# Half of the last block of an expert's second weights, loaded one step early and copied in place, in the expert loop of a GNN and mixture-of-experts kernel

## The chip, the cores and the metric

The kernel runs on one core of a Trainium2 chip. The metric is the device time of one execution in microseconds (us); lower is better. The work is in float32.

## The reference, cut to what matters

A two-layer graph attention network is added to 625 rows of 768 features. Then come causal attention and a mixture of eight experts, of which each row uses one (K = 1, so its gate weight is 1). Only the last part is touched by the change:

```python
h2 = _ln(x, ln2_g, ln2_b).reshape(-1, d)
gate_logits = h2 @ Wg
w, sel = jax.lax.top_k(gate_logits, K)              # K = 1
...
hid = jax.nn.relu(jnp.einsum('nd,edf->enf', h2, W1) + b1[:, None, :])   # 768 -> 3072
y = jnp.einsum('enf,efd->end', hid, W2) + b2[:, None, :]                # 3072 -> 768
moe = jnp.einsum('ne,end->nd', combine, y)
return x + moe.reshape(b, t, d)
```

## The kernel before, in words

**Rows by expert.** After attention, each of five tiles of 125 rows is normalised, its expert chosen, and its rows are scattered by expert into two DRAM buffers: `xg` (the normalised rows) and `xr` (the sum so far, and the row's number). The expert that most rows of the first tile chose is the first expert; its weights are loaded and its first 128 rows are worked on in a step written out ahead of the loop (step A), between whose products the last routing work runs.

**The table.** About forty small VectorE operations on one partition then make a table of 21 columns with four rows: expert, whether it is new, kind of step, first row in `xg` and `xr`. A step has kind 0, 1 or 2 for M = 128, 64 or 32 rows. An expert's rows are cut into at most one step of 32, at most one of 64 and then some of 128, in that order. The engines read the words they need from the table at the start of a loop step (`values_load`), and branch on the kind with `tc.If`, so the code of a step is there three times.

**One step** (`step`, L1075). P = 128 / M groups of hidden columns are worked on side by side. `into(c)` (L1091) multiplies the turned rows `xbT` with a chunk of W1 into PSUM `ph`, and VectorE copies it to `hb` (L1095). `turn(c)` (L1102) transposes it on TensorE, and ScalarE adds the bias and applies ReLU into `hbT` (L1107). `out_of(c)` (L1114) multiplies `hbT` with a chunk of W2 and accumulates in PSUM `py`, for two halves i of 384 output columns. TensorE's order is written out by hand (`manual_schedule`). For M = 64 and M = 32 there are n = 3 chunks, and it is: into 0, into 1, turn 0, into 2, turn 1, out 0, turn 2, (transposes `tpx` of the next step's rows, L891) out 1, (more `tpx`) out 2. In a step of 32, `out_of(c)` has K = 2 slices of 128 hidden rows for each of 4 groups; group g reads slices 2g and 2g + 1 of block c. So its first two products read the first half of `w2[c]`, and the third and the fourth the second half. After the last product VectorE adds `py` to `yo` (which holds `xr`'s rows plus the bias b2, L1156 to L1158) at L1166, and GpSimd scatters `yo` to the output (L1168).

**The weights.** W1 and W2 of an expert lie in SBUF once, each as three blocks, `w1[0..2]` and `w2[0..2]`, of 3 MB; there is no second buffer. `load_expert(e, new)` (L1066) is called at the end of a step for the next step's expert: twelve transfers of 1.5 MB, two for each block (L1037 for W1, L1031 for W2), with the bias b2 (L1043) in the middle, all on SyncE's queue in the order w1[0], w1[1], w1[2], b2b, w2[0], w2[1], w2[2]. Where the next step has the same expert, the condition `new` is 0: SyncE still goes through the instructions and their waits, and no bytes move. Each transfer waits until TensorE has read the old contents, and for the eighth transfer before it on the same queue (eight completion semaphores are used in turn). SyncE's order is written out by hand as well.

**Per step on the other queues.** GpSimd loads the next step's rows (`xb`, L1340, always 128 rows) and this step's sums (`rb`, L1058, always 128 rows), and VectorE copies the step's first-layer bias (L1064).

The lines that matter most, of `out_of` and of the adds at the end:

```python
for k in range(K):
    for i in range(2):
        for g in range(P):
            mm = nc.tensor.matmul(py[g * M:(g + 1) * M, i, :384], hbT[c][:, k, g * M:(g + 1) * M],
                                  w[:, o + g * K + k, i * 384:(i + 1) * 384], ...)
...
for g in range(P):
    for cc in range(4 // P):
        nc.vector.tensor_add(yv[:, :, cs], yv[:, :, cs], py[g * M:(g + 1) * M, :, cs])
```

Of the kernel before, what the change touches and what calls it, by code (L numbers as in the profile page):

```python
# [9 lines left out]
F32 = mybir.dt.float32  # L10
F16 = mybir.dt.float16
BF16 = mybir.dt.bfloat16
I32 = mybir.dt.int32
# [11 lines left out]
D = 768  # L25
# [37 lines left out]
def gnn_moe_kernel(ctx: ExitStack, tc: tile.TileContext, p, out):  # L63
# [83 lines left out]
    with tc.tile_pool(name="gnn", bufs=1) as gp:  # L147
# [322 lines left out]
        sx = ctx.enter_context(tc.tile_pool(name="sx", bufs=1, side="right", reuse_waits="tile"))  # L470
# [214 lines left out]
    table = keep.tile([1, 4, NS + 1], I32, name="table")  # L685
    first = keep.tile([1, 1], I32, name="first")
    sxt = ctx.enter_context(tc.tile_pool(name="sxt", bufs=1, side="right", reuse_waits="tile"))
# [339 lines left out]

    def load_piece(e, l, c, **cond):
        if l:
            for k in range(0, FC // 128, 4):  # L1030
                nc.sync.dma_start(  # L1031
                    w2[c][:, k:k + 4, :],
                    W2[ds(e, 1), c * FC + k * 128:c * FC + (k + 4) * 128, :]
                    .rearrange("o (k p) d -> p (o k) d", p=128), **cond)
        else:
            for k in range(0, KD, 3):
                nc.sync.dma_start(  # L1037
                    w1[c][:, k:k + 3, :],
                    W1[ds(e, 1), k * 128:(k + 3) * 128, c * FC:(c + 1) * FC]
                    .rearrange("o (k p) f -> p (o k) f", p=128), **cond)  # L1040

    def load_bias(e, **cond):
        nc.sync.dma_start(b2b, b2[ds(e, 1), :].to_broadcast([B, D]), **cond)  # L1043
# [12 lines left out]
    def sums_so_far(row):  # L1056
        rb = mw.tile([B, D + 1], F32, name="rb", bufs=1)
        nc.gpsimd.dma_start(rb, xr[ds(row, B), :])  # L1058
        return rb

    def biases(e):
        bT = mw.tile([128, NK], F32, name="bT")
        of_e = bT_all.rearrange("p (e k) -> p e k", k=NK)[:, ds(e, 1), :]
        return bT, nc.vector.tensor_copy(bT, of_e.rearrange("p o k -> p (o k)"))  # L1064

    def load_expert(e, new):  # L1066

        with tc.manual_schedule(engines={SP}):
            for l in range(2):
                for c in range(NFC):  # L1070
                    load_piece(e, l, c, cond=new)
                if not l:
                    load_bias(e, cond=new)

    def step(M, xT, bT, rb, after=None):  # L1075
# [33 lines left out]
        def out_of(c):  # L1109
            w, o = (w2[c // 2], (c % 2) * K) if P == 1 else (w2[c], 0)  # L1110
            for k in range(K):
                for i in range(2):
                    for g in range(P):
                        mm = nc.tensor.matmul(  # L1114
                            py[g * M:(g + 1) * M, i, :384], hbT[c][:, k, g * M:(g + 1) * M],
                            w[:, o + g * K + k, i * 384:(i + 1) * 384],
                            start=(c == 0 and k == 0), stop=(c == n - 1 and k == K - 1))
            return mm
# [43 lines left out]
        for g in range(P):  # L1162
            for cc in range(4 // P):
                w = 384 * P // 4
                cs = slice(cc * w, (cc + 1) * w)
                nc.vector.tensor_add(yv[:, :, cs], yv[:, :, cs], py[g * M:(g + 1) * M, :, cs])  # L1166
# [138 lines left out]
    v.tensor_copy(tabf[:, 0, :NS], its_number)  # L1305
    v.tensor_copy(table, tabf)
# [8 lines left out]
    row_0 = nc.values_load(table[0:1, 3, 0:1], engines=[pool], min_val=0, max_val=NR - B)  # L1315
    first_rows = nc.gpsimd.dma_start(xb, xg[ds(row_0, B), :])
    first_turned, = step_a

    def next_expert(i):
        return (nc.values_load(table[0:1, 0, ds(i, 1)], engines=[SP], min_val=0, max_val=E - 1),  # L1320
                nc.values_load(table[0:1, 1, ds(i, 1)], engines=[SP], min_val=0, max_val=1))

    load_expert(*next_expert(0))

    def all_of(step, e, new):
        with tc.manual_schedule(engines={PE}):
            for _ in step:
                pass
        load_expert(e, new)
# [3 lines left out]
    with tc.For_i(0, n_blk, 1, iteration_sync="reg_based") as i:  # L1333
        e = nc.values_load(table[0:1, 0, ds(i, 1)], engines=[mybir.EngineType.DVE], min_val=0,
                           max_val=E - 1)
        kind = nc.values_load(table[0:1, 2, ds(i, 1)], min_val=0, max_val=2)
        row, row_next = (nc.values_load(table[0:1, 3, ds(k, 1)], engines=[pool], min_val=0,
                                        max_val=NR - B) for k in (i, i + 1))

        nc.gpsimd.dma_start(xb, xg[ds(row_next, B), :])  # L1340
        rb = sums_so_far(row)
        bT, s = biases(e)
        tc.add_manual_dep(s.ins, first_rows.ins.name, ORDER)

        then = next_expert(i + 1)
        with tc.If(kind == 0) as cmp:
            all_of(step(B, xbT, bT, rb, first_turned), *then)
        with cmp.Else():
            with tc.If(kind == 1) as cmp2:
                all_of(step(64, xbT, bT, rb, first_turned), *then)  # L1350
            with cmp2.Else():
                all_of(step(32, xbT, bT, rb, first_turned), *then)
# [31 lines left out]
```

## Time and profile before

| what | value |
|---|---|
| time, three runs | 1070.33, 1070.99 (median), 1072.49 us |
| the profiled execution's own time | 1070.6 us |
| its span in the profile | 1067.9 us |
| TensorE busy | 1006.7 us (94% of the span) |
| VectorE, ScalarE, GpSimd busy | 451.7, 319.0, 57.1 us |
| step A | from 627.9 us |
| the expert loop | 700.1 to 1060 us |
| bytes moved by DMA | 194.48 MB, mean 182 GB/s |

The steps of the loop, from TensorE's timeline (start of the first `into` product) and from the times at which transfers of weights run. "New" means that the step's expert was not the expert of the step before, so that its weights were loaded during the step before:

| step | rows M | starts (us) | weights |
|---|---|---|---|
| 1 | 64 | 700.13 | as in step A |
| 2 | 128 | 736.35 | the same |
| 3 | 64 | 801.68 | new, loaded in step 2 |
| 4 | 32 | 840.54 | new, loaded in step 3 |
| 5 | 128 | 866.12 | the same |
| 6 | 64 | 931.47 | new, loaded in step 5 |
| 7 | 32 | 965.72 | new, loaded in step 6 |
| 8 | 64 | 993.27 | the same |
| 9 | 32 | 1027.52 | new, loaded in step 8 |

How to read it: the page's slices show how busy each engine was over the span, and the granted TensorE clock. A group row gives busy time and mean duration, then the idle time ahead of it on its engine and what ended that. A timeline row gives start, duration, engine, line, operation, tiles, shapes, count, and in brackets the idle time before it with its releaser. The engine named SPq is SyncE's sequencer, which issues the transfers of weights.

### The profile page before, as it was taken

How to read it: one execution, taken by the hardware profiler on the slowest of the kernel's cores; microseconds unless marked ns; L12 is line 12 of the kernel's file. 1: busy time of each engine (PE TensorE's matmuls, PEld its weight loads, DVE VectorE, ACT ScalarE, POOL GpSimd, SP SyncE). 2: the span in 40 equal slices, each digit the busy share in tenths (PEclk: the TensorE clock that was granted, in tenths of full speed). 3: DMA queues.
4: the chain of work that ended last, by engine and by line, in shares of the span. 5: the costliest groups of instructions: out<-in, count | busy, mean ns of one | idle time of the engine just before them, and what ended most of it. 6: DMA issues, size and time to landing. Idle time of an engine off the chain costs nothing. (4 is left out here: it accounts for less than half of the span.)

```text
span 1067.9 us, 14435 instructions
## 1 busy us (share of the span) xinstructions
PE 1006.7 (94%) x4763; PEld 574.8 (54%) x4764; DVE 451.7 (42%) x1264; ACT 319.0 (30%) x817; POOL 57.1 (5%) x97
## 2 busy tenths in 40 slices
PE   6889999999999999999999999999999889998993
PEld 4455465677656556666665654544453435533341
DVE  6886786484284910665438544011101121011211
ACT  6677553452231111444435211110202112021120
POOL 1200100000000100000001101000000000000000
PEclk9999999999999999999999999999999899998997
DMA  9300500301300347998002679012799948899693
GB/s 286 129 1 1 181 9 0 133 1 43 93 14 0 103 120 220 398 389 293 1 2 63 237 251 351 12 46 58 304 321 387 408 177 322 294 413 409 248 412 153
DMA packets 85669, 194.48 MB, mean 182 GB/s; under 512 B 32397, under 2 KB 34068, under 8 KB 85609
## 3 DMA queue, kind: packets, MB, share of 16 engines
q1 hardware_dynamic: 79817, 174.00, 44.3%
q0 software_dynamic: 5712, 19.54, 5.3%
q8 instruction: 36, 0.59, 0.2%
q10 hardware_dynamic: 80, 0.16, 0.1%
q14 instruction: 24, 0.20, 0.1%
HBM read 251.98 MB, written 38.37 MB: 272 GB/s over the span
## 5 line engine op out<-in xcount | busy, mean ns | idle before, releaser
L1114 PE MATMUL py<-ew,hbT 128*64 128x384 f32 (+2 forms) x960 | 196.0, 517 | 12.8 <-DMA ew<-in_L_ffn_W_dram 12.8
L1091 PE MATMUL ph<-ew,xbT 128*32 128x256 f32 (+2 forms) x864 | 153.9, 499 | 7.8 <-issue 4.5
L1114 PEld LDWEIGHTS py<-ew,hbT 128*64 128x64 f32 (+2 forms) x960 | 91.6, 149 | 97.7 <-issue 62.3
L1107 ACT ACTIVATE hbT<-tph,bT 128x64 f32<-128x64 f32 (+2 forms) x240 | 55.3, 333 | 264.2 <-PE tph L1102 162.3
L1091 PEld LDWEIGHTS ph<-ew,xbT 128*32 128x32 f32 (+2 forms) x864 | 63.9, 135 | 87.2 <-issue 79.9
L1166 DVE TENSOR_TENSOR yo<-yo,py 64x384 f32<-64x384 f32 (+2 forms) x40 | 23.0, 608 | 182.9 <-PE py L1114 182.5
L1095 DVE COPY hb<-ph 128x512 f32<-128x512 f32 (+1 forms) x39 | 24.5, 629 | 149.8 <-PE ph L1091 149.8
L528 PE MATMUL agg<-xl,zT 125*125 125x256 f32 (+1 forms) x300 | 79.8, 417 | 1.3 <-ACT zT L517 1.1
L528 PEld LDWEIGHTS agg<-xl,zT 125*125 125x125 f32 x300 | 54.5, 188 | 19.6 <-ACT zT L517 2.6
L231 ACT ACTIVATE step<-iota,past 125x314 f16<-125x314 f16 x120 | 55.9, 548 | 0.0
L356 PE MATMUL pp<-w,yT 128*125 128x512 f32 x120 | 55.3, 600 | 0.0
L628 PE MATMUL ph<-wr,h1T 128*125 128x384 f32 x160 | 52.8, 486 | 0.0
L590 PE MATMUL ph<-w,h1T 128*125 128x384 f32 x160 | 52.4, 486 | 0.0
L837 ACT ACTIVATE e<-e,nm 125x125 f32<-125x125 f32 (+4 forms) x60 | 36.0, 602 | 39.5 <-DVE nm L834 39.5
L248 PE MATMUL cps<-step,oh 125*125 125x314 f16 x181 | 37.4, 309 | 10.5 <-ACT step L231 5.4
L900 PE MATMUL po<-wpj,aT 128*125 128x384 f32 x120 | 44.3, 499 | 1.2 <-DVE nm L834 0.7
L241 DVE TENSOR_SCALAR oh<-iota,drel,upper 125x125 f16<-125x125 f16 x160 | 41.2, 317 | 3.4 <-PE cps L248 3.4
L166 PE MATMUL ph<-wr,yT 128*125 128x512 f32 x96 | 42.1, 593 | 0.1
L590 PEld LDWEIGHTS ph<-w,h1T 128*125 128x125 f32 x160 | 30.0, 188 | 21.2 <-issue 0.5
L628 PEld LDWEIGHTS ph<-wr,h1T 128*125 128x125 f32 x160 | 29.8, 187 | 20.8
L808 PE MATMUL pq<-hT,L_ffn_Wq 128*128 128x313 f32 (+1 forms) x144 | 40.9, 432 | 0.0
L834 DVE CUSTOM_DVE_ANT_0 e<-sc,later 125x125 f32<-125x125 f32 (+4 forms) x60 | 30.7, 544 | 24.1 <-PE sc L828 23.9
(328 smaller groups left out, 1248.9 us busy)
## 6 DMA issues: line engine op xcount, KB each, us to landing
ew<-in_L_ffn_W_dram SPq DMA_DIRECT2D x132, 1536.0 KB
xr<-zt SPq DMA_DIRECT2D x5, 3076.0 KB
xg<-zt SPq DMA_DIRECT2D x5, 3072.0 KB
w<-in_L_gnn_W_dram SPq DMA_DIRECT2D x4, 1536.0 KB
wr<-in_L_gnn_Wr_dram SPq DMA_DIRECT2D x4, 1536.0 KB
b2b<-in_L_ffn_b_dram SPq DMA_DIRECT2D x11, 384.0 KB
xb<-xg POOLq DMA_DIRECT2D x10, 384.0 KB, 6.1
rb<-xr POOLq DMA_DIRECT2D x9, 384.5 KB, 7.0
```

Source lines behind the costliest of these rows:

```text
L166: nc.tensor.matmul(pp[:R, :], yT[:, c, cols(t)], part(wr1, KD, c, i, 512), start=(c == 0), stop=(c == KD - 1))
L231: nc.scalar.activation(o, iota[:, :SH + 1], AF.Sign, bias=at, scale=-1.0)
L241: m = nc.vector.tensor_scalar(o, iota[:, :n], at, weight, op0=OP.is_equal, op1=OP.mult)
L356: nc.tensor.matmul(pp[:R, :], yT[:, c, cols(t)], part(w1, KD, c, i, 512), start=(c == 0), stop=(c == KD - 1))
L528: nc.tensor.matmul(self.agg[:R, c0:c0 + n], zT[:, s, :], xl[:, s, x0:x0 + n], start=(s == 0), stop=(s == T - 1))
L590: nc.tensor.matmul(ph[:R, :384], h1T[:, c, cols(t)], part(w2, KH, c, i, 384), start=(c == 0), stop=(c == KH - 1))
L628: nc.tensor.matmul(ph[:R, :384], h1T[:, k, cols(t)], part(wr2, KH, k, i, 384), start=(k == 0), stop=(k == KH - 1))
L808: nc.tensor.matmul(pp[:, :b - a], w[:, c, c0:c0 + 128], hT[:, c, a:b], start=(c == 0), stop=(c == KD - 1))
L900: mm = nc.tensor.matmul(pp[:R, i, :384], aT[:, c, cols(t)], wpj[i][:, c, :], start=(c == 0), stop=(c == KD - 1))
L1091: mm = nc.tensor.matmul(ph[g * M:(g + 1) * M, :C], xT[:, k, :M], w[:, k, o + g * C:o + (g + 1) * C], start=(k == 0), stop=(k == KD - 1))
L1107: nc.scalar.activation(hbT[c][:, k, r], tp[:, k, r], AF.Relu, bias=bT[:, f:f + 1])
L1114: mm = nc.tensor.matmul(py[g * M:(g + 1) * M, i, :384], hbT[c][:, k, g * M:(g + 1) * M], w[:, o + g * K + k, i * 384:(i + 1) * 384], start ...
```

## The change

Five edits, all in the expert part:

- **Ahead.** The second half of the last W2 block, `w2[2]`, of a new expert is no longer loaded by `load_expert`. A tile `ahead` of 1.5 MB takes it. It is loaded early in the step before (`load_ahead`, on SyncE's queue ahead of that step's `load_expert`), and at the start of the next step ScalarE copies it into `w2[2]`. The copy is made in every step, new or not. The tile lies where two pools of the right side (`sx`, `sxt`) lay, which are now closed before the loop; the load for the loop's first step is unconditional.
- **One word.** Expert, kind, next expert and next new flag are packed into one table word (expert x 128 + new x 64 + next expert x 8 + next new x 4 + kind), read once per step by each engine and unpacked with shifts and masks. The table has two rows in place of four.
- **Column halves.** In the last `out_of` of a step, all products of output columns 0 to 383 come before those of columns 384 to 767.
- **Adds by halves.** The adds into `yo` are split likewise: eight adds of half the size in place of four.
- **Sums by M.** `rb` is loaded with M rows in place of 128, and so within the branch.

```diff
+    def load_half(to, e, c, k, **cond):
+        nc.sync.dma_start(to, W2[ds(e, 1), c * FC + k * 128:c * FC + (k + 4) * 128, :]
+                          .rearrange("o (k p) d -> p (o k) d", p=128), **cond)
     def load_piece(e, l, c, **cond):
         if l:
-            for k in range(0, FC // 128, 4):
-                nc.sync.dma_start(w2[c][:, k:k + 4, :], ...)
+            for k in range(0, FC // 128 - (4 if cond and c == NFC - 1 else 0), 4):
+                load_half(w2[c][:, k:k + 4, :], e, c, k, **cond)
...
-    def sums_so_far(row):
+    def sums_so_far(row, M):
         rb = mw.tile([B, D + 1], F32, name="rb", bufs=1)
-        nc.gpsimd.dma_start(rb, xr[ds(row, B), :])
+        nc.gpsimd.dma_start(rb[:M], xr[ds(row, M), :])
...
+    def load_ahead(e, **cond):
+        load_half(ahead, e, NFC - 1, FC // 128 - 4, **cond)
...
         def out_of(c):
-            for k in range(K):
-                for i in range(2):
-                    for g in range(P):
-                        mm = nc.tensor.matmul(...)
+            order = [(k, i) for k in range(K) for i in range(2)]
+            for k, i in sorted(order, key=lambda o: o[1]) if c == n - 1 else order:
+                for g in range(P):
+                    mm = nc.tensor.matmul(...)
...
-        for g in range(P):
-            for cc in range(4 // P):
-                nc.vector.tensor_add(yv[:, :, cs], yv[:, :, cs], py[g * M:(g + 1) * M, :, cs])
+        for i in range(2):
+            for g in range(P):
+                for cc in range(4 // P):
+                    nc.vector.tensor_add(yv[:, i, cs], yv[:, i, cs], py[g * M:(g + 1) * M, i, cs])
...
-    v.tensor_copy(tabf[:, 0, :NS], its_number)
-    v.tensor_copy(table, tabf)
+    a = tabf[:, 0, :]
+    v.scalar_tensor_tensor(a[:, :NS], its_number, 2.0, tabf[:, 1, :NS], op0=OP.mult, op1=OP.add)
+    w = tabf[:, 2, :NS]
+    v.scalar_tensor_tensor(w, a[:, 1:], 4.0, w, op0=OP.mult, op1=OP.add)
+    v.scalar_tensor_tensor(w, a[:, :NS], 64.0, w, op0=OP.mult, op1=OP.add)
+    v.tensor_copy(table, tabf[:, 2:, :])
...
-    load_expert(*next_expert(0))
+    right.close()
+    ahead = ctx.enter_context(tc.tile_pool(name="ahp", bufs=1, reuse_waits="tile")).tile(
+        [128, 4, D], F32, name="ahead")
+    word_0 = word(0, SP)
+    with tc.manual_schedule(engines={SP}):
+        load_ahead((word_0 >> 7) & 7)
+    load_expert((word_0 >> 7) & 7, (word_0 >> 6) & 1)
...
     with tc.For_i(0, n_blk, 1, iteration_sync="reg_based") as i:
+        w = word(i)
+        kind, then = w & 3, ((w >> 3) & 7, (w >> 2) & 1)
         nc.gpsimd.dma_start(xb, xg[ds(row_next, B), :])
-        rb = sums_so_far(row)
-        bT, s = biases(e)
+        nc.scalar.copy(w2[NFC - 1][:, FC // 128 - 4:, :], ahead)
+        load_ahead(then[0], cond=then[1])
+        bT, s = biases((w >> 7) & 7)
-        then = next_expert(i + 1)
+        def part(M):
+            all_of(step(M, xbT, bT, sums_so_far(row, M), first_turned), *then)
```

## The prediction

> **What bounds the kernel now.** First the page: TensorE is busy almost throughout, and the group of W2 products is the costliest one whose idle time a transfer ends; the adds into `yo` wait for it.
>
> ```profile
> PE   6889999999999999999999999999999889998993
> PEclk9999999999999999999999999999999899998997
> L1114 PE MATMUL py<-ew,hbT 128*64 128x384 f32 (+2 forms) x960 | 196.0, 517 | 12.8 <-DMA ew<-in_L_ffn_W_dram 12.8
> ```
>
> The reader is to see the slices that dip in the last third, in both rows. TensorE's timeline shows which steps they are. It is read next, for the W2 products of steps 4, 7 and 9 (M = 32):
>
> ```profile
> 858.13 0.84 PE L1114 MATMUL py<-ew,hbT 128*32 128x384 f32 x4
> 861.72 4.47 PE L1114 MATMUL py<-ew,hbT 128*32 128x384 f32 x28 [2.75 <-DMA ew<-in_L_ffn_W_dram]
> ...
> 974.50 2.79 PE L1114 MATMUL py<-ew,hbT 128*32 128x384 f32 x32
> ...
> 978.76 0.84 PE L1114 MATMUL py<-ew,hbT 128*32 128x384 f32 x4 [0.51 <-DMA ew<-in_L_ffn_W_dram]
> 982.70 5.33 PE L1114 MATMUL py<-ew,hbT 128*32 128x384 f32 x28 [3.10 <-DMA ew<-in_L_ffn_W_dram]
> ...
> 990.56 2.77 PE L1114 MATMUL py<-ew,hbT 128*32 128x384 f32 x28 [1.26 <-DMA ew<-in_L_ffn_W_dram]
> ```
>
> Four products of a chunk run, then the other 28 wait for the second half of the block. A chunk of 32 takes 2.79 us, so 28 take 2.45 at full clock; after waits of 2.75 and 3.10 us they took 4.47 and 5.33, after 1.26 only 2.77. Pieces become usable 3.93 us apart (982.70 to 990.56 is two). Step 9 shows the same (1040.36, 1044.54, 1052.39). Then the stages by windows, from step 6 into step 8:
>
> ```profile
> 936.00:966.00 30.00, 30.00 (x174) 12.07 (x174) 3.13 (x6) 6.08 (x26) 1.10 (x2) 1.00 1.02 414
> 982.00:989.00 7.00, 6.30 (x34) 2.02 (x34) 0.00 (x0) 0.36 (x1) 0.00 (x0) 0.55 1.03 401
> 993.00:998.00 5.00, 5.00 (x25) 1.64 (x24) 3.97 (x5) 0.00 (x0) 0.00 (x0) 1.00 0.00 0
> ```
>
> The last three columns are granted clock, DMA share and GB/s. Through steps 6 and 7 the transfers run at full rate (414 GB/s), and the clock falls to 0.55 behind the wait. At the start of step 8 they stand idle. So steps of 32 rows that follow a step of 64 end with the transfers; all other steps end with TensorE. Last, the chain of waits:
>
> ```profile
> 1052.39 2.80 PE py L1114 x28
> ...
> 1055.21 0.95 DVE yo L1166
> ...
> 1058.15 0.97 DVE yo L1166
> ```
>
> Four adds, 3.95 us with their gaps, stand behind the last product, bare.
>
> **Ahead, steps 3 and 4, 6 and 7.** The transfer moves from last in an expert's load to first. The bytes are the same, so only its start counts. Before, in step 6, the last piece of the old load was issued at 931.7 (SyncE's lines), when step 5's products ended, and held the queue for 3.93 us; the first W1 piece was issued at 935.8 and came right behind. After, that last piece is gone (it was taken during step 5, whose start has idle transfers), and `ahead` waits for the copy: 931.5 + 2.9 = 934.4. The copy of 3072 columns costs 2.9 us by the SBUF reads of 625 and 250 columns at 815 and 498 ns (0.85 ns per column); bounds are 2.8 (the 1000-column copy at 998 ns, same slope as 625 at 677) and 4.5 (250 columns at 364 ns, scaled whole). SyncE is there in time: its old turnaround from step to step took 4.2 us (801.9 to 806.0, three table reads of 0.7 each), and it now starts when out(4) of step 5 frees the first half, about 5 us earlier. So the load starts about 1.0 us earlier than the old one. `rb` of 64 and 32 rows in place of 128 saves 0.20 + 0.30 MB, at 410 GB/s 1.2 us. The last landing moves by -2.2, and every other piece, one slot later in the queue, by 3.93 - 2.2 = +1.7.
>
> Step 4: the first half of w2[2], now the last to be used, was usable at 861.72 - 3.93 = 857.8 and is at 859.5. TensorE, after its 4.55 us gap at the step's start (unchanged), is there at 858.5 and waits 1.0, too short for the clock to fall. Then 32 products: 859.5 + 2.8 = 862.3, where it was 866.2. That is **-3.8** (-2.6 without the saving of `rb`; -4.3 at best, with TensorE as the bound).
>
> Step 7: pieces at 976.5 (second half of w2[0]), 980.5, 984.4 and 988.3. TensorE waits 1.7 at out 0, 0.5 at out 1, then 3.6 until 984.4; 28 products with a fallen clock take 5.3 (row above): 989.7. Transposes 0.5, 32 products 2.8: 993.0, where it was 993.3: **-0.3**. The gain at the last piece is eaten by the clock, since the long wait now comes later. Bounds: +0.9 without `rb`'s saving, -2.2 if the clock holds (then 988.3 + 2.8).
>
> **Ahead, steps 8 and 9.** Here transfers stood idle until the first W1 piece at 998.07: in step 7 SyncE was held by the landing at 990.5, since its skipped transfers wait for their turn of semaphores, then skipped eight more and turned. Now the copy ends at 993.35 + 2.9, `ahead` goes out at 996.3, 1.8 us earlier; with `rb`'s 1.2 the last landing moves by -3.0 and the others by +0.9. Step 9: 1044.54 + 0.9 = 1045.4, a wait of 3.9, 5.3 + 0.5 + 2.8: 1054.0 for 1055.2. That is **-1.2** (+0.3 without `rb`'s saving and with slow transposes; -3.0 if the clock holds).
>
> [...]
>
> **Column halves and adds.** One add of 384 columns takes 0.548 us (the 64x384 form), 0.565 with its gap; eight are 4.5. The first four run while the second half's 16 products run (1.4 us): 4.5 - 1.4 = 3.1 behind the last product, for 3.95: **-0.8** (-0.7 to -1.0), at the program's end alone. Elsewhere the next step's products cover the adds. The order of products by columns costs nothing: each product still loads its own weights (960 and 960), and `into`, which stays in one bank, runs at the same 0.86 ns per column.
>
> **Loop entry.** TensorE stood idle 1.35 us before step 1, released by SyncE's loop entry at 699.9. SyncE came from the skipped transfer into the second half of w2[2], which waits for step A's last product (698.8). That transfer is gone; the one left is free about 5.3 us earlier. VectorE's entry (699.4) is late next: **-0.6** (0 to -1.3).
>
> **Costed at nothing.** The copy lies on ScalarE at the step's start; its next work, `hbT`, comes 5.8 us in at the earliest (965.8 to 971.66). Without that cover it would cost 2.9 per step. The packing adds some small VectorE operations before 660 us, 40 us ahead of the loop. The first `ahead` moves in step A, 683 to 690, where the DMA share is 0 to 0.01. On SyncE two reads fewer per step save 1.4 us; shifts and masks add three to five register instructions per transfer, estimated at 0.2 to 0.4 us each by FUSED_REGOPS (168 ns) and ALU_OP (33 ns): in a load they hide behind a queue of seven pieces, and in step 7 the nine skips after the landing end at about 995.5, before the copy does. GpSimd's `rb` sits behind a branch, 0.4 us later; its reader runs 14 us before the adds.
>
> **Sum.** -0.6 - 3.8 - 0.3 - 1.2 - 0.8 = -6.7, from the profiled execution's 1070.6 (0.4 below the median of the runs, 2.7 above its span): 1063.9. The ends add to 1058.9 and 1069.0.
>
> **Rivals.** *Slower: SyncE is held by its own code.* Every step branches into one of three copies, and SyncE's listing grows from 208 to 363 rows. The price is the gap at step 4's first entry into new code, 4.55 us with full queues (1.90 at step 2 with idle ones). One such stop per step hides in steps 3 and 6 behind SyncE's early arrival (930.1 + 4.55 is 934.7), and costs step 9 its gain: 1045.4 + 4.6, then 8.6 as before, is 1058.6, +3.4; the sum is -2.1, 1068.5. Two per step put `ahead` at 939.2 in place of 934.5: step 4 +0.9, step 7 (989.1 + 8.6) +4.4, step 9 +8.0, in all +11.9 and 1082.5. It decides from about 5 us of added delay per step. Against it: steps 3 to 9 show turnarounds of 3.5 to 4.2 us with no such stop, and TensorE, with far more code, stops only at first entries. [...]
>
> *No change: the queue is full anyway.* If the copy takes 4.5 us and `rb`'s bytes don't count, the last landing stays, and each of three steps runs 32 products behind it in place of 28 (+0.3): -0.6 - 0.8 + 0.9 = -0.5, 1070.1. For it: the same bytes at the same 414 GB/s.
>
> *A larger gain: the clock holds.* If the waits at 984.4 and 1045.4 don't lower the clock, -0.6 - 3.8 - 2.2 - 3.0 - 0.8 = -10.4, 1060.2. Against it: 2.75 and 3.10 were enough before.
>
> **How the numbers follow.** The forecast has 0.50, one stop per step 0.09, the clock that holds 0.15, the full queue 0.13, two stops 0.13. What a measurement of this kernel can tell from no change is about 0.2%, 2.1 us: under 1068.9 counts as faster. Faster: 0.50 + 0.15 + 0.09 and 0.01 from the full queue, 0.75; same 0.12; slower 0.13. The range runs from the clock that holds to the full queue, 1060.0 to 1070.2, and leaves out the two stops and a few below.
>
> **What would show it.** Right: step 4's last W2 products as 32 in a row near 859.5 after a wait of about 1 us; in steps 7 and 9 a wait at out 0 that was not there, a longer one at the second half of out 1, none at out 2; `ahead` issued about 3 us into steps 3, 6 and 8; 3.1 us of adds at the end; no gap of 1.35 before step 1. Wrong: `ahead` issued later than 5 us into a step, transfers below 400 GB/s in steps 3, 6 and 8, or `hbT` waiting for the copy.

## The result, and the profile after

| | before | after |
|---|---|---|
| time, median of 12 executions each, side by side | 1071.13 us | 1070.66 us (1069.72 to 1073.62) |
| ratio after to before, 95% interval | | 0.9998 (0.9986 to 1.0010) |
| the profiled execution, its span | 1070.6, 1067.9 us | 1073.1, 1071.0 us |
| end of step A's products to the end of the last add | 360.3 us | 360.2 us |

No difference that can be measured; 1063.9 was predicted. The profiled execution after is 3 us longer than the one before, but its step A ended at 702.0 us in place of 698.8, in code that the change does not touch (over all profiles here this point lies between 698.4 and 703.8). So the text below compares the stretch from the end of step A's products, the last row of the table.

First the page of the changed kernel, the rows that were shown of before:

```profile
PE   6889999999999999999999999999999899997993
PEclk9999999999999999999999999999999999999997
L1122 PE MATMUL py<-ew,hbT 128*64 128x384 f32 (+2 forms) x960 | 192.7, 503 | 14.7 <-DMA ew<-in_L_ffn_W_dram 14.7
```

The W2 products got shorter in sum (192.7 us for 196.0: of the groups of 28 products behind a wait three were slow before, 4.47 to 5.33 us, and two are after, 4.46 and 4.36), but wait more for transfers (14.7 for 12.8). TensorE's timeline, W2 products of steps 4 and 7 (start, duration, ..., idle time before and its releaser):

```profile
858.60 0.84 PE L1122 MATMUL py<-ew,hbT 128*32 128x384 f32 x4
861.09 2.77 PE L1122 MATMUL py<-ew,hbT 128*32 128x384 f32 x28 [1.66 <-DMA ew<-in_L_ffn_W_dram]
...
864.95 2.79 PE L1122 MATMUL py<-ew,hbT 128*32 128x384 f32 x32 [0.72 <-DMA ew<-in_L_ffn_W_dram]
...
976.16 0.84 PE L1122 MATMUL py<-ew,hbT 128*32 128x384 f32 x4
979.40 2.89 PE L1122 MATMUL py<-ew,hbT 128*32 128x384 f32 x28 [2.41 <-DMA ew<-in_L_ffn_W_dram]
...
983.81 0.84 PE L1122 MATMUL py<-ew,hbT 128*32 128x384 f32 x4 [0.71 <-DMA ew<-in_L_ffn_W_dram]
987.74 4.46 PE L1122 MATMUL py<-ew,hbT 128*32 128x384 f32 x28 [3.09 <-DMA ew<-in_L_ffn_W_dram]
...
992.51 2.79 PE L1122 MATMUL py<-ew,hbT 128*32 128x384 f32 x32
```

Most of the pattern is the predicted one: a wait at out 0 of step 7 that was not there, none at out 2, and step 4 is 2.5 us shorter and ends with 32 products in a row after a wait of 0.7 us. The wait at the second half of out 1 in step 7 did not get longer (3.09 us for 3.10), and step 4 has one at out 1 too, of 1.66 us, which the prediction did not have. And every piece is later than predicted: the wait at out 0 of step 7 is 2.41 us for 1.7. The windows over the same stages (granted clock, DMA share and GB/s last):

```profile
937.00:967.00 30.00, 30.00 (x170) 12.10 (x166) 2.99 (x5) 6.10 (x26) 1.10 (x2) 1.00 1.01 381
994.00:999.00 5.00, 4.91 (x35) 1.85 (x28) 3.36 (x7) 2.75 (x1) 0.00 (x0) 1.00 0.00 0
```

Step 6 ran its transfers at 414 GB/s before; now 381 in the 30 us after they start, under the 400 that the prediction named as the sign that it is wrong. Step 8's transfers still start after 999: `ahead` goes out 3.75 us into that step, not 3.0. And the chain of waits, its first and last add:

```profile
1057.60 0.55 DVE yo L1175
...
1061.66 0.57 DVE yo L1175
```

The last product ends at 1057.45. All eight adds stand behind it. The gap before step 1, which was to go, is 1.57 us.

### The profile page after: what moved, and what is told of

Read it like the earlier page. It is cut to its first block, busy times and chain, and to the rows that moved or that the text cites. A ratio compares the mean times of both kernels' runs of the same rounds, so it can differ in the third digit from the quotient of the medians.

```text
span 1071.0 us, 14972 instructions
## 1 busy us (share of the span) xinstructions
PE 1006.0 (94%) x4763; PEld 576.6 (54%) x4764; DVE 456.4 (43%) x1306; ACT 344.3 (32%) x826; POOL 57.1 (5%) x97
## 4 chain that ended last, share of the span: by engine, by line
PE 66%; DVE 6%; DMA 6%; issue 4%; SPq 3%; ACT 1%; POOL 1%; POOLq 0%; DVEq 0%; ACTq 0%
PE py L1122 14%; PE ph L1098 14%; PE pq L809 7%; PE agg L529 6%; DMA ew<-in_L_ffn_W_dram 6%; PE ph L591 5%; PE ph L629 3%; PE pv L772 3%; PE ph L166 3%; SPq L1030 3%; PE sc L829 2%; PE o L870 2%; PE po L901 2%; PE tpe L852 1%; PE tph L1109 1%
## 5 line engine op out<-in xcount | busy, mean ns | idle before, releaser
L1122 PE MATMUL py<-ew,hbT 128*64 128x384 f32 (+2 forms) x960 | 192.7, 503 | 14.7 <-DMA ew<-in_L_ffn_W_dram 14.7
L1175 DVE TENSOR_TENSOR yo<-yo,py 64x192 f32<-64x192 f32 (+2 forms) x80 | 27.3, 378 | 182.0 <-PE py L1122 180.9
L248 PEld LDWEIGHTS <-oh 125*125 125x125 f16 x181 | 26.1, 147 | 28.2 <-DVE oh L241 13.9
```

The costliest lines, as they stand in the source:

```text
L248: nc.tensor.matmul(where, target(R, d[:, j:j + 1], w[:, j:j + 1]), step(s[:, j:j + 1], j % 4 != 3), start=False, stop=False, skip_group_ch ...
```

## The experiments

Each edit is against the changed kernel unless said otherwise. The lengths are from one profile of each, from the start of a step to the start of the next (step 9: to the end of its last product; steps 3 and 4 are added since an idle gap at the start of step 4, told of below, comes and goes). "Adds" is the time from the last product to the last add, "sum" the whole stretch from step A's products to the last add. Time and ratio are medians of 6 to 12 executions beside before (1071.1 to 1072.4 us in those sets); where there is no ratio, it is one execution, and only its steps are read. The changed kernel stands there twice (also as g3): steps 3 and 4, 7 and 9 of its two profiles differ by 0.2, 0.5 and 0.4 us, so smaller differences between two profiles say nothing.

| run | steps 3+4 | 7 | 9 | adds | sum | time, ratio (95%) |
|---|---|---|---|---|---|---|
| before | 64.4 | 27.6 | 27.6 | 3.9 | 360.3 | |
| changed kernel | 62.2 | 28.1 | 27.8 | 4.8 | 360.2 | 1070.7, 0.9998 (0.9986 to 1.0010) |
| g3_after_again | 62.4 | 28.6 | 27.5 | 4.7 | 359.8 | 1070.8, 0.9991 (0.9978 to 1.0003) |
| e1_rb128 | 62.0 | 28.8 | 27.6 | 4.8 | 360.4 | 1071.7 |
| e2_no_rb | 60.7 | 26.6 | 26.8 | 4.8 | 355.8 | 1066.6 |
| e3_rb_wide | 61.5 | 26.9 | 27.1 | 4.8 | 357.1 | 1067.4 |
| e4_py_split | 61.4 | 27.8 | 27.8 | 3.4 | 357.7 | 1067.7, 0.9971 (0.9956 to 0.9987) |
| f1_ahead_alone | 61.7 | 27.8 | 27.6 | 4.0 | 358.5 | 1068.6, 0.9958 (0.9943 to 0.9973) |
| h4_ahead_again | 61.8 | 27.7 | 27.7 | 4.0 | 358.4 | 1068.3, 0.9972 (0.9955 to 0.9988) |
| h1_halves | 62.1 | 29.2 | 27.7 | 4.8 | 360.3 | 1070.9, 0.9995 (0.9982 to 1.0008) |
| h2_narrow | 62.4 | 26.9 | 26.7 | 4.0 | 356.4 | 1068.9, 0.9965 (0.9950 to 0.9979) |
| h3_halves_split | 61.9 | 27.4 | 27.5 | 3.4 | 357.3 | 1068.6, 0.9969 (0.9956 to 0.9983) |
| i1_whole128 | 62.7 | 27.6 | 25.8 | 4.8 | 360.6 | 1070.8, 0.9991 (0.9971 to 1.0011) |
| f2_rb_sp | 59.9 | 24.9 | 29.7 | 3.9 | 354.9 | 1066.4, 0.9942 (0.9920 to 0.9963) |
| g1_rb_act | 61.8 | 27.0 | 27.1 | 3.4 | 356.2 | 1067.6, 0.9968 (0.9956 to 0.9980) |
| f3_best | 62.1 | 24.4 | 29.7 | 3.9 | 358.8 | 1066.1, 0.9928 (0.9905 to 0.9952) |
| g2_filled | 62.4 | 28.2 | 27.2 | 4.7 | 359.8 | 1070.5, 0.9993 (0.9979 to 1.0006) |
| g4_best2 | 62.6 | 27.0 | 27.0 | 3.4 | 357.2 | 1067.3, 0.9962 (0.9947 to 0.9978) |
| f4_order64 | 62.1 | 28.4 | 27.7 | 4.8 | 361.2 | 1075.7 |

### What became of rb's saving: e1, e2, e3

**e1_rb128**: `rb` with 128 rows again, still in the branch.

```diff
-        nc.gpsimd.dma_start(rb[:M], xr[ds(row, M), :])
+        nc.gpsimd.dma_start(rb, xr[ds(row, B), :])
```

> The changed kernel, with the sums rb loaded with 128 rows again (still inside the branch). Theory A (the prediction's term: fewer bytes save queue time, 1.2 us for the rows of a step of 64 and a step of 32 together): every piece of weights in steps 4, 7 and 9 lands about 1.2 us later than in the changed kernel, and the three steps get longer by 0.5 to 1.2 us each (from 23.1, 28.1 and 27.8 us). Theory B (a narrow load of 64 or 32 rows holds up the queues as long as 128 rows, since the trace of the changed kernel shows the rate at 250 to 280 GB/s for 3 us behind each load of 64 rows while the share stays at 1.0): those dips go, the landings move by less than 0.4 us, and the three steps keep their lengths within 0.4 us.

**e2_no_rb**: `rb` is loaded once, ahead of the loop. As the rows' numbers come with `rb`, every step then scatters to the rows of the loop's first step, here and in e3.

```diff
+    rb_once = sums_so_far(row_0, B)
...
-            all_of(step(M, xbT, bT, sums_so_far(row, M), first_turned), *then)
+            all_of(step(M, xbT, bT, rb_once, first_turned), *then)
```

> The changed kernel with the sums rb loaded once ahead of the loop and not in the steps (each step adds the sums of the loop's first rows, so the output is not the reference's). It shows what the loads of rb cost the weights. Theory A (only bytes count): 0.29 MB fewer between the start of the load and the last landing, so landings 0.7 us earlier in steps 4, 7 and 9. Theory B (the narrow loads hold up the queues): the dips behind the steps of 64 rows (about 0.46 MB not moved, 1.1 us) go as well, landings 1.8 to 2.2 us earlier; step 7 falls from 28.1 to about 26.5, step 9 from 27.8 to about 26.5.

**e3_rb_wide**: as many bytes as the narrow load, but spread over 128 partitions.

```diff
+            n = B // M
+            nc.gpsimd.dma_start(rb_once[:, :D // n],
+                                xg[ds(row, M), :].rearrange("r (h c) -> (r h) c", h=n))
```

> As the run without rb, but with a load of the same size as the narrow rb in its place (64 or 32 rows of xg), spread over all 128 partitions as half or quarter rows, into columns of the sums tile (the output is not the reference's). [...] Theory B2 (the dip comes from the number of rows, or from GpSimd's path whatever the form): the dips of 250 to 280 GB/s stay, landings as in the changed kernel.

Measured: with 128 rows again, steps 4, 7 and 9 are 0.3 shorter, 0.7 longer and 0.2 shorter (step 4 alone 22.8 for 23.1): no gain from the narrow load. With no load at all they are 1.4, 1.5 and 1.0 shorter. The same bytes over 128 partitions give 0.7, 1.2 and 0.7 of that. So in the wide form the bytes saved are worth something: the three steps are 0.5, 1.9 and 0.5 us shorter than with 128 rows, where 1.2, 1.2 and 1.5 were predicted (1.0 of the 1.9 is the clock: 28 products in 4.13 us for 5.12). The narrow form loses it again. Where it does so is seen in windows of 1 us behind `rb`'s issue in step 6. The changed kernel:

```profile
945.00:946.00 1.00, 1.00 (x8) 0.41 (x6) 0.00 (x0) 1.00 (x6) 0.00 (x0) 1.00 1.00 250
946.00:947.00 1.00, 1.00 (x7) 0.29 (x4) 0.00 (x0) 0.06 (x1) 0.00 (x0) 1.00 1.04 283
```

And the wide load at the same place:

```profile
941.30:942.30 1.00, 1.00 (x8) 0.41 (x6) 0.00 (x0) 1.00 (x6) 0.00 (x0) 1.00 1.03 404
942.30:943.30 1.00, 1.00 (x8) 0.29 (x4) 0.00 (x0) 0.06 (x1) 0.00 (x0) 1.00 1.03 410
```

The DMA engines count as busy in both (share 1.0), but behind the load of 64 partitions they move 250 to 283 GB/s for two to three microseconds where the stream otherwise has 410. It is not the length of the rows, which is halved in e3: e1 loads 128 rows as long as those of the narrow load and has 400 and 401 GB/s at this place. Why a narrow load slows the others' packets was not tried.

### The adds by halves: e4, and the load ahead by itself

**e4_py_split**: each half of `py` is a tile of its own.

```diff
-        py = sp.tile([128, 2, 512], F32, name="py", bufs=1)
+        py = [sp.tile([128, 512], F32, name=f"py{i}", bufs=1) for i in range(2)]
```

> The changed kernel with the accumulator py as two tiles, one for each half of the output columns. Theory T1 (the adds wait for all of py, since the wait is kept for a tile as a whole; the trace of the changed kernel has all eight adds behind the last product): now the first four run beside the second half's products; behind the last product of step 9 stand 3.2 us in place of 4.8, the time falls by 1.6 us, and steps 1 to 9 keep their lengths. Theory T2 (VectorE reaches the adds late for another reason, its own queue or the sums): the tail stays at 4.8 us.

The chain of waits of that run, at its end:

```profile
1050.28 1.59 PE py L1122 x16
...
1051.90 0.55 DVE yo L1175
```

The first add now starts when 16 of the last 32 products are done, and the last add ends 3.44 us behind the last product in place of 4.77. In the changed kernel the first add of the first half reads the same tile that the second half's products still write, and waits for the last of them. But 1.3 us is not all that the split gave: the median is 3 us lower (0.9971 of before, where the changed kernel has 0.9998). So the edits were put on the load ahead one by one.

**f1_ahead_alone**, and once more as **h4_ahead_again**: the load ahead, the copy and the table word; the rest as before.

```diff
-            for k, i in sorted(order, key=lambda o: o[1]) if c == n - 1 else order:
+            for k, i in order:
...
-        nc.gpsimd.dma_start(rb[:M], xr[ds(row, M), :])     # in the branch
+        nc.gpsimd.dma_start(rb, xr[ds(row, M), :])         # M = 128, ahead of the branch
...
-        for i in range(2):                                 # eight adds of half the size
+        for g in range(P):                                 # four adds, as before
```

> Of the five edits only the load ahead, the copy, and the one table word stay; sums with 128 rows ahead of the branch, products and adds in the order of before. Theory: the load ahead shortens steps 3 and 4 together by about 2.3 us and lengthens step 7 by 1.0 (the wait at the second half of the middle block comes later and the clock falls behind it), step 9 within 0.3; the last adds take 4.0 us behind the last product as before. Sum about -1.3: 1070 us, hardly to be told from no change. Rival (the load ahead is worth nothing at all, all that was seen in step 4 is scatter): 1071.3, with step 4 at 25.6 us.

> The load ahead alone once more beside these: 1068.6 us, 0.995 to 0.998 of before. Rival (its gain of the first time was the chip's or the clock's): 1070 us, under 0.2% from before.

**h1_halves**: f1 with the column halves, `py` one tile. **h2_narrow**: f1 with the narrow `rb` in the branch. **h3_halves_split**: h1 with `py` in two tiles.

> The load ahead (with the copy and the one table word), and the products and adds by column halves on one py tile; rb with 128 rows ahead of the branch as before. Theory (the adds by halves cost 0.8 us, since the first half's adds wait for the last product of both): 0.8 us slower than the load ahead alone: the adds end 4.8 us behind the last product. 1069.4 us. Rival (the halves cost nothing, the narrow load does): as the load ahead alone, 1068.6.

> The load ahead, and rb with M rows inside the branch; products and adds whole, as before. Theory (the narrow load behind the branch takes its bytes back through a slower stream): 0.5 to 1.2 us slower than the load ahead alone, in steps 4, 7 and 9; 4.0 us behind the last product. 1069.4 us. Rival (the halves alone make the difference): as the load ahead alone, 1068.6.

> As the first of these runs with py in two tiles: the adds end 3.4 us behind the last product. 0.6 us faster than the load ahead alone: 1068.0 us. Rival (no such overlap): 1069.4.

The load ahead alone is faster than before in both sets (together with the copy and the table word, which were not tried apart). On the same chip, the halves on one tile cost 2.6 us of it (1070.9 for 1068.3, and no longer distinguishable from before). Two tiles give 2.3 back, which is not more than the load ahead alone has, though the adds end 0.6 us sooner. As h3 has the same order of products as h1, that order is not what costs. The narrow `rb` costs 0.6, within the scatter of the runs. (In h2's profile steps 7 and 9 are 0.8 and 0.9 shorter than in h4, against its theory; but that execution has the shortest span of its twelve, 3.3 us under their median, so its steps say little.) So the halves on one tile undid the gain; the expectation, 0.8, was too small. Of h1's longer stretch, 0.7 is in the adds and 1.5 in step 7: there the weights for the second half of out 1 are usable 0.9 us later (54.84 us behind the start of step 6 for 53.96), and the 28 products behind that wait took 5.33 us for 4.84, a matter of the clock. What step 7 lost on the weights began in step 6. The load ahead alone, h4: GpSimd's and SyncE's timelines and two windows of 1 us, the fourth and fifth of step 6 (which starts at 929.71):

```profile
931.89 1.03 POOL L1176 DMA_INDIRECT out_dram<-yo,idx  x1 [58.93 <-DVE bT L1067]
...
932.75 0.38 SPq L1030 DMA_DIRECT2D ahead<-in_L_ffn_W_dram  x1
...
932.71:933.71 1.00, 1.00 (x8) 0.38 (x6) 0.00 (x0) 0.01 (x1) 0.21 (x1) 1.00 0.24 98
933.71:934.71 1.00, 1.00 (x8) 0.34 (x6) 0.00 (x0) 0.00 (x0) 0.20 (x1) 1.00 1.22 283
```

With the halves on one tile, h1 (step 6 starts at 930.79):

```profile
933.23 1.02 POOL L1177 DMA_INDIRECT out_dram<-yo,idx  x1 [58.45 <-DVE bT L1067]
...
933.83 0.38 SPq L1030 DMA_DIRECT2D ahead<-in_L_ffn_W_dram  x1
...
933.79:934.79 1.00, 1.00 (x8) 0.38 (x6) 0.00 (x0) 0.01 (x1) 0.46 (x1) 1.00 0.00 0
934.79:935.79 1.00, 1.00 (x8) 0.34 (x6) 0.00 (x0) 0.00 (x0) 0.00 (x0) 1.00 0.68 68
```

`ahead` is issued 3.04 us into the step in both. But the scatter of the step before is issued at 2.18 in h4 and at 2.44 in h1, since eight adds on 128 rows take longer than four (1.40 us in the changed kernel, 1.15 in f1); it ends at 3.21 in h4, before SyncE's issue of `ahead` ends (3.42), and at 3.46 in h1, after it. In h1 nothing moves in the fourth microsecond, and from 2 to 14 us into the step 0.30 MB less arrive than in h4 (0.7 us at 410 GB/s). Whose bytes they are is seen by queue (packets, MB, share of the 16 engines): q0 has the transfers that GpSimd issues, q1 the weights. The fourth and fifth microsecond of h4:

```profile
q0 software_dynamic: 66, 0.37, 69.7%
q1 hardware_dynamic: 4, 0.01, 3.3%
```

The sixth and seventh of h1 (935.79:937.79), in which h4 moves 0.66 MB of weights:

```profile
q1 hardware_dynamic: 113, 0.35, 53.9%
q0 software_dynamic: 59, 0.32, 38.8%
```

So what moves early in h4 is the scatter itself. Its first packets run 0.57 us behind the end of its issue and nearly all of them before the weights, whose first packet comes 4.62 us into the step. In h1 the scatter's first packets run 2.06 us behind the end of its issue, 5.53 us into the step, and its bytes take their place from the weights. The first packet of `ahead` is not late (4.09), but 1.5 MB of weights have moved only 10.56 us into step 6, in h4 9.66. The changed kernel, e1, e2 and e3 all have the scatter at 2.44 and a zero in the fourth microsecond, in steps 3 and 6; e4 and h3, with `py` in two tiles, have the scatter at 1.78 and 240 to 258 GB/s there.

**i1_whole128** takes the later scatter away in steps 3 and 6 only.

```diff
-        for i in range(2):
+        for i in [slice(0, 2)] if P == 1 else [0, 1]:
```

> The changed kernel, with the adds of steps of 128 rows whole again (four of 192 columns by two halves in place of eight), and by halves in the other steps. Steps 3 and 6 follow steps of 128 rows. Theory (in steps 3 and 6 the adds by halves put GpSimd's scatter of the step before from 2.18 us to 2.44 us into the step; it then ends at 3.46, behind SyncE's issue of the load ahead at 3.04 to 3.42, and the load's first bytes move 1 us later): scatter back at 2.18, bytes of the load ahead in the fourth microsecond of steps 3 and 6, which had none; steps 4 and 7 each 0.5 to 1.0 us shorter than in the changed kernel (23.1 and 28.1 to 28.6), step 9 and the 4.8 us behind the last product as they were. 1069.3 us. Rival (the order of products or adds costs otherwise, the scatter's place doesn't matter): steps 4 and 7 within 0.3 of the changed kernel, 1070.7.

The place is confirmed: scatter at 2.18, the fourth microsecond moves 98 GB/s (the scatter's own bytes, not those of the load ahead that the theory named), and from 2 to 14 us into step 6 0.40 MB more arrive than in the changed kernel. The second half of out 1 in step 7 is usable 53.8 us after the start of step 6 where the changed kernel had 54.7. The total is not better, because the edit has a price of its own, which was not expected:

```profile
994.45 1.08 PE L1098 MATMUL ph<-ew,xbT 128*64 128x512 f32 x4 [0.94 <-DVE yo L1175]
```

The first products of steps 7, 8 and 9 wait 0.67, 0.94 and 0.67 us for an add of the step before, and that of step 5 waits 0.91; no other run has these waits. The waits ahead of steps 5 and 8 count in steps 4 and 7: without them these take 22.7 and 26.6 us, 0.4 and 1.5 less than in the changed kernel. Step 9, which was to stay, is 2.0 shorter; `ahead` went out 2.6 us into the late step 8, not 3.75. (The copies of the step's code now differ in their number of VectorE instructions, which may be why; that was not tried.) In this profile the clock fell in step 2 as well, +1.7 us. By its time alone this run would have spoken for the rival.

### rb out of the stream: f2 and g1

**f2_rb_sp**: e4, and `rb` with 128 rows on SyncE's queue, ahead of `ahead`. **g1_rb_act**: e4, and `rb` on ScalarE's queue behind the copy.

```diff
         with tc.manual_schedule(engines={SP}):      # f2
+            rb = sums_so_far(row, B)                # nc.sync.dma_start
             load_ahead(then[0], cond=then[1])
```

> The sums' two PSUM halves are separate tiles, and the sums so far (rb) are loaded with 128 rows on SyncE's queue at the start of the step, ahead of the load ahead, while the transfers stand idle, in place of the narrow load by GpSimd in mid-stream. Theory (the narrow load holds up the stream of weights for 1.3 us or so in each of steps 3, 6 and 8): steps 4, 7 and 9 each 0.8 to 1.5 us shorter than with the separate tiles alone, no stretch behind the first pieces under 350 GB/s; 1064.5 us. Rival (the bytes count wherever they are): nothing gained or lost, 1067.7.

> The two halves of py as separate tiles, and rb with 128 rows on ScalarE's queue right behind the copy, about 3.5 us into the step, ahead of nearly all weights. Theory (in mid-stream GpSimd's narrow load costs more than its bytes; on SyncE's queue rb held up SyncE's start, 6.2 us into step 8 for the load ahead): steps 4 and 7 as with rb on SyncE's queue (20.8 and 24.9 us) within 0.6, step 9 about 27.5 in place of 29.7, the load ahead in step 8 issued 5 us in. 1065.0 us. Rival (what held step 9 back was the order of the transfers, not SyncE's start): step 9 stays at 29 to 30 us, 1066.5.

f2 has steps 3+4 and 7 at 59.9 and 24.9, the shortest but for f3's step 7, and loses 1.9 in step 9: step 7 has become so short that SyncE, which still goes through its skipped transfers, issues `rb` 5.0 and `ahead` 6.2 us into step 8. On ScalarE's queue `ahead` goes out at 4.7 and step 9 takes 27.1, as its theory said, but steps 3+4 and 7 are 2 us longer than f2's. What costs these was not pursued, and g1's theory failed there. f2 gains most so far: 1066.4, 0.6% under before.

### The clock: f3, g2, g4

**f3_best**: f2, and in steps of 32 rows groups 0 and 1 of a chunk before groups 2 and 3.

```diff
-            for k, i in ...:
-                for g in range(P):
+            gs = [range(2), range(2, 4)] if P == 4 and c < n - 1 else [range(P)]
+            for part, (k, i) in [(a, o) for a in gs for o in order]:
+                for g in part:
```

> As the run before, and in a step of 32 rows the products of groups 0 and 1 of a chunk, which read the first half of the block, come before those of groups 2 and 3. Two groups side by side take twice the time per product (8 products of each of two groups about 2.7 us, where 32 of four groups take 2.8), so TensorE works through most of the 3.1 us wait. Theory (the clock falls because TensorE is idle for over 2.7 us): the granted clock stays at 1.0 in step 7 and 9, and the 28 products that took 4.4 us become 16 in 2.7; another 0.5 to 1.0 us off steps 7 and 9 each, until the last landing bounds them: 1063.3 us. Rival (the fall of the clock isn't tied to the wait): products as slow as before, and the halved side-by-side costs 2 us per chunk: 1066 to 1068.

**g2_filled**: five transposes that nobody reads, in out 1 of steps of 32 rows. **g4_best2**: the same on top of g1.

```diff
+                    if M == 32 and c == 1 and (k, i, g) == (0, 0, 1):
+                        spare = sp.tile([128, 4, 128], F32, tag="tp", name="spare")
+                        for a in range(5):
+                            nc.tensor.transpose(spare[:, a % 4, :], ident, ident)
```

> The changed kernel with five transposes that nobody reads (0.22 us each) on TensorE in every step of 32 rows, between the products of the middle block's first half and those of its second. Theory: the clock is set for each stretch of a fixed grid of 3.41 us, and falls for one stretch when TensorE was busy for less than about 0.41 of the stretch before; in steps 7 and 9 of the changed kernel that share was 0.19 and 0.15. With 1.1 us more work it is about 0.5: the clock stays at 1.0 and the 28 products take 2.8 in place of 4.4 us. Step 7 then is 27.2 in place of 28.1 and step 9 27.0 in place of 27.8, bound by the last landing; step 4 within 0.3. About -1.7 against the changed kernel. Rival (the fall follows from the length of the wait for the transfer, whatever TensorE does in between, or the transposes stand in the way): 0 to +1.1.

> py in two tiles, rb on ScalarE's queue, and the five spare transposes. Theory: as the first of these runs, with the clock at 1.0 where it falls there: another 0.5 to 1.5 us, 1064.0. Rival (with rb out of the way the waits are short and the transposes only add work): 1065.5 to 1066.

f3's clock held in steps 7 and 9, and step 7 became the shortest of all (24.4); but in step 4, where TensorE did not wait, a chunk in two parts takes 4.10 us in place of 2.79, and steps 3+4 lost 2. By their times f3 and f2 can't be told apart (0.9928 and 0.9942, intervals that overlap; f3's profile also has a fall of the clock in step 2, +1.7 us). The five transposes were too small: pipelined, they took 0.76 us in all, not 1.1, TensorE's share of the stretch was 0.31, and the clock fell as before. g2 equals the changed kernel, g4 equals g1. Which shares were followed by a fall is in the last section.

### The loop entry: f4

**f4_order64**: the copies of the step's code in another order.

```diff
-        with tc.If(kind == 0) as cmp:
-            part(B)
+        with tc.If(kind == 1) as cmp:
+            part(64)
```

> The changed kernel with the copies of the step's code in another order: 64 rows first, then 128, then 32. Theory (the idle time ahead of steps 1 and 4 is TensorE's branch into code that it has not run yet): step 1 now falls through, its gap of 1.6 us falls to under 0.8, and step 2, which now has to branch, has a gap of 2 to 4 us where it had 2.2. Rival (SyncE or VectorE's loop entry releases step 1): the gap ahead of step 1 stays at 1.1 to 1.6 us. The time is 1070 to 1073 by both.

The branch of TensorE's sequencer at the loop entry, from its source line (duration in ns), and the first product behind it. The changed kernel:

```profile
L1370 PEldq COMPARE_BRANCH  x1: 3884/3884/3884, 699.1 to 699.1; - x1
...
703.59 10.52 PE L1098 MATMUL ph<-ew,xbT 128*64 128x512 f32 x48 [1.57 <-issue]
```

With the code of 64 rows first:

```profile
L1370 PEldq COMPARE_BRANCH  x1: 93/93/93, 700.9 to 700.9; - x1
...
704.52 1.94 PE L1098 MATMUL ph<-ew,xbT 128*64 128x512 f32 x8 [0.75 <-DVEq L1354]
```

The branch takes 93 ns in place of 3884, and the gap halves; VectorE's loop entry is late next. The 4.8 us gap at step 4 is gone as well, while TensorE stopped for 3405 and 3537 ns at other entries, beneath queued products. The gain is not seen in the sum (this execution's clock fell in step 2, +1.7 us, and steps 3+4 end with the transfers either way).

**g3_after_again** is the changed kernel once more, for the comparison on one chip:

> The changed kernel once more, beside the others on the same chip. By the sum of its steps it is 1.7 us slower than the load ahead alone and 2.5 slower than with py in two tiles: 1070.5 us, 0.998 to 1.000 of before. Rival (the gains over before seen with the other kernels are the chip's): as fast as these, under 1069.

It came out as said: 0.9991 of before, and 3.2 us behind g1 on the same chip (1070.8 for 1067.6). The load ahead alone ran on other chips; by the sum of its stretch the changed kernel is 1.3 us behind it here.

## Why the prediction was wrong, step by step

| term | predicted | measured |
|---|---|---|
| loop entry | -0.6 | +0.23 |
| steps 3 and 4 | -3.8 | -2.25 |
| step 7 | -0.3 | +0.56 |
| step 9 | -1.2 | +0.18 |
| adds at the end | -0.8 | +0.83 |
| step 1, not counted on | 0 | +0.34 |
| sum | -6.7 | -0.11 |

**Right.** The load ahead does what was said: `ahead` issued 3.0 us into steps 3 and 6, the copy 2.75 us (2.9 predicted) and never in `hbT`'s way, the last landing in step 6 moved by -1.2 with the load ahead alone (58.3 us after the start of step 6 before, 57.1 in f1 and h4) where -1.0 was predicted without `rb`. By itself it is worth 1.8 us by its steps, and 0.3 to 0.4% by its medians. SyncE did not stop in its code: its COMPARE_BRANCH rows are 0.14 us at most.

**The step that failed most: "`rb` of 64 and 32 rows in place of 128 saves 0.20 + 0.30 MB, at 410 GB/s 1.2 us".** It counted bytes. e1 shows that the narrow load gives none of it: the last weights that TensorE waits for in steps 4 and 7 are usable 59.31 and 54.77 us behind the starts of steps 3 and 6 with 128 rows, and 59.48 and 54.72 with the narrow load. In a wide load as many bytes give 0.5 and 0.9 us of it (58.80 and 53.89 in e3). All three terms that leaned on it (1.2, 1.2 and 1.5 us of the 6.7) came out near the bound that the prediction had set "without `rb`'s saving": -2.6, +0.9, +0.3. For steps 7 and 9 that is luck in part. The weights behind the long wait were usable 20.47 and 20.37 us into these steps, forecast were 18.7 and 17.9: 1.8 and 2.5 later, more than `rb`'s 1.2. The 28 products behind the wait gave 0.8 and 0.9 of it back, as they took 4.46 and 4.36 us, not 5.3.

**"The first four run while the second half's 16 products run."** They don't: +0.8 for -0.8. The reads wait by tile, not by half: on one tile the first add starts 0.15 us behind the last product (1057.60 and 1057.45); with a tile for each half the adds end 3.44 us behind the last product, -0.5 (e4). And "elsewhere the next step's products cover the adds" overlooked who else waits for them: GpSimd's scatter, whose bytes then moved amid the weights and not ahead of them (h1, h4, i1). The prediction named `rb` on GpSimd's queue, but not the scatter in front of it.

**"Released by SyncE's loop entry."** The profile names the last semaphore. SyncE reached its loop entry at 697.4, 4.6 us ahead of the end of step A's products, where it had come 1.1 behind (699.9 and 698.8 before), and nothing was gained: TensorE was in its branch until 703.0, 1.0 us behind these products (before 699.4, 0.6 behind). f4 shows what is there without the branch, 0.75 us. The prediction's rival put stops of that kind on SyncE, where no branch took over 0.14 us; they are TensorE's, whose rows at the entries to steps 1 and 4 are 3.9 and 5.9 us, the first while 4 GB/s moved and the second while 404 did. What holds TensorE there, and why the other engines' branches take 0.16 us at most, no run here shows.

**"28 products with a fallen clock take 5.3".** They took 4.46 here, 5.33, 4.84 and 2.77 in other runs behind waits of the same 3.1 us. It was a draw, not a price. (At full clock 28 products take 2.77 us by the prediction's own rows, not its 2.45, and the ends of its terms add to 1058.8 and 1068.5, not to 1058.9 and 1069.0; the forecast uses none of these.)

The "full queue" rival came nearest in its number (1070.1), and half for its reason: `rb`'s bytes did not count, but the copy was not slow, and most of what the load ahead gave the last landing was taken by the scatter's bytes.

## What to carry to other kernels

Price a smaller transfer by its shape as well as by its bytes, and look at the rate of the stream beside it (here 250 to 283 GB/s behind the load of 64 partitions, 404 and 410 behind as many bytes over 128). When an edit makes the end of a step later under the cover of the next one, follow every queue that waits for that end: here a scatter that was issued 0.26 us later moved amid the weights, and the first 1.5 MB of these were through 0.65 and 0.9 us later (h1 against h4, steps 3 and 6). Splitting the work was of use here only where the tile that synchronises it was split too (the adds ended 4.8 us behind the last product on one tile, 3.4 on two, 3.9 to 4.0 unsplit), and of five edits made together one may undo another: the load ahead alone (0.9958 and 0.9972), or the change with `py` in two tiles and `rb` ahead of the weights (0.9942), beats the change as it was made.

## What the runs showed of the hardware

**The clock changed on a fixed grid.** In every profile here the stretches of half clock within the loop begin on one grid of 3.413 us and last one or two of its cells. In the changed kernel they begin at 845.03, 988.39 and 1049.83 us, 42 and 18 cells apart, and last one cell each; before, at 838.08, 861.98, 981.44 and 1042.88 us, 7, 35 and 18 cells apart, they last two, one, two and two. Cells of the grid in the changed kernel's step 7 (TensorE's busy time is the second number, the clock the third from the end):

```profile
984.98:988.39 3.41, 0.65 (x9) 0.34 (x13) 0.00 (x0) 0.00 (x0) 0.00 (x0) 1.00 1.02 399
988.39:991.80 3.41, 3.41 (x24) 1.28 (x16) 0.00 (x0) 0.00 (x0) 0.00 (x0) 0.50 0.68 266
```

And in f2, behind a wait of the same 3.09 us that the grid cuts in two:

```profile
980.13:983.54 3.41, 1.95 (x25) 0.97 (x27) 0.00 (x0) 0.00 (x0) 0.00 (x0) 1.00 1.03 402
983.54:986.95 3.41, 2.65 (x30) 1.14 (x28) 0.55 (x2) 0.37 (x1) 0.00 (x0) 1.00 0.53 204
```

A cell in which TensorE was busy for 0.19 of the time was followed by half clock, one with 0.57 was not. Over the 19 profiles, from 700 to 1052 us, 62 of 63 cells at full clock with a share up to 0.42 were followed by half clock, and 181 of 182 with 0.44 to 0.97 were not. At half clock the 23 cells up to 0.69 stayed, the 57 from 0.80 on did not. So a wait of 3.1 us cost nothing, one cell or two, by where it fell: in step 7 the granted clock stayed at 1.00 in f2, and the 28 products behind the wait took 4.46 us in the changed kernel and 5.33 before.

**The scatter's bytes came late where `ahead` was issued before the scatter's own issue ended.** In steps 3 and 6 SyncE issues `ahead` from 3.04 to 3.42 us. Where the scatter's issue ends at 2.8 or 3.2 us, its first packets run 0.57 us later and it lands 3.4 to 3.6 us after its start (e4, f1, h2, h3, h4, i1). Where it ends at 3.46, they run 1.8 to 2.5 us later, amid the weights, and it lands after 5.3 to 5.9 us (the changed kernel, e1, e2, e3, h1). What holds them back was not tried.

**The gap at TensorE's first entry into the code of 32 rows came and went from build to build.** It is 4.5 to 4.9 us at step 4 in fifteen of the profiles; there is none in e4, f4, g1 and h2, whose programs differ in other lines, so that the layout of the code may be the cause, which was not shown. Where it is gone, the transfers end steps 3 and 4 nearly as late: 61.4 (e4) against 62.2.
